# Output stage of a four-layer image network: spreading factors through masked copies and one product, row sums on VectorE, and both offsets' taps in one product

## Chip, cores and metric

The kernel runs on one core of a Trainium2 chip. The metric is the device time of one execution in microseconds (us), from one launch with all inputs in HBM to the output in HBM; the median over several executions is given. All data are float32.

## What is computed

The input is a batch of 4 images of 56 x 56 positions and 128 channels. Four layers follow one another:

- Layer 0: attention in shifted windows, attention over the whole image, and a two-layer perceptron.
- Layer 1: for each row of positions, sums of relu over all pairs of positions, then a linear layer with relu.
- Layer 2: an attention layer whose projections are spectral convolutions. It takes a sample as 56 images, one for each place t on the first axis, each of 56 (second axis) x 128 (channels) values. Its end is what matters here: each such image gets `attention = inorm(projd + xa)`, then `m = gelu(inorm(spec(inorm(attention))) + skip)`, `m = inorm(spec(m)) + skip`, and the output `inorm(m) + attention`. `inorm` takes mean and variance over one image's 56 x 128 values, so it has one factor for each t.
- Layer 3: a convolution with three taps along one image axis, and sums of its result over each axis.

Between layers 2 and 3 lies a normalization over groups of 4 channels, so layer 3's input is `r * (x - m)` per channel. Layer 3, cut to what matters:

```
y = conv(xc, W, taps along the first image axis, zero padding) + b
agent_sum = sum(y, axis=3)          # over the second image axis
time_sum  = sum(y, axis=2)          # over the first image axis
g = (agent_sum + time_sum - y) / sqrt(56 + 56 - 2)
out = relu(g + res)                 # res: the layer's input
```

A convolution of sums is the sum of the convolution, so the kernel convolves the sums of the input (`whole.nl`, over the second axis; `whole.na`, over the first) in place of summing the result. A sum over the first axis, shifted by one tap, lacks one edge row of the image: this is where the "row sums" of the change come in.

## The kernel before

Layers 0 to 2 run ahead of the stage that is changed. From about 3239 us on, `outputs` (L2624) does the end of layer 2 and the whole of layer 3. It works on four samples; each sample has two halves of 28 of its 56 images (`half_sample`, L2069), and then `last_layer` (L2431) runs once for the sample.

Both functions do not issue instructions at once. They add operations to a `Plan`: an operation has an engine, an estimated cost, the operations it comes after, and the buffers that it takes and gives back. `plan.issue` (L2048) then runs all 788 of them in the sequence `OUTPUT_ORDER` (L2591), a list of numbers written out in the source. Within an engine the instructions execute in that sequence, for TensorE, ScalarE, VectorE and GpSimd; between engines only semaphores order them. The change leaves the list as it is.

Buffers: `bank()` is one PSUM bank out of two (tag "b"), `banks()` a pair out of three (named `o_d`). GpSimd does not read PSUM here, so what it takes is copied by VectorE or ScalarE first.

**Spreading the factors.** In `half_sample` a tile is [128 partitions (channels), 28 images (T), 56 (second axis)]. An image belongs to one of four slots (t modulo 4) and one of seven groups (G = 7). `sums` forms the sums of squares of the images of slot s into partitions 32s to 32s + 31; `root` takes the square root on ScalarE and the reciprocal on VectorE (L2210). So one factor for each image stands in a small tile [128, G], in a different partition block for each slot. `everywhere` (L2213 to 2231) brings them to all 128 partitions. For each slot it multiplies with a stationary matrix `w.slot[:, s, :]`, which is 1 in the row 32s and 0 elsewhere:

```
for s in range(4):
    nc.tensor.matmul(ps[:, s * n * G:(s + 1) * n * G], w.slot[:, s, :],
                     V[src].rearrange("p x g -> p (x g)"), start=True, stop=True)
```

`copies` (L2229) then scales the result from PSUM into one value for each image. It happens twice for each half, 16 times in all:

- After `inverses` (L2303 the reciprocal, L2305 the small tile `o_e`), with two factors an image (n = 2). They become `f1` for `normed` (L2357, GpSimd) and `fs` for `skip` (L2317, GpSimd: `a = att * fs`).
- After the reciprocal of `r5` (L2210), with one factor an image. It becomes `f5` for `last` (GpSimd), behind which `sum2` (GpSimd) adds the half into the sample `whole.x`.

In between, `under` (L2312, VectorE) makes the factor `f` from `o_e`. L2110, L2127 and L2141 are the products of `over_h`, `over_c` and `over_w`; L2179 is the addition in `weighted` (GpSimd).

**The last layer.** For each sample: `aggregate` and `means` (L2462) and `variances` (L2475) give mean and variance of the channel groups; `root` takes the square root; `scale` takes the reciprocal (L2483) and multiplies the three tap matrices with it (`wr`, L2485). `over_l` (L2487 to 2495) forms on TensorE the sum of both halves of `whole.na`, three times in one PSUM bank, less an edge row for the first and the last tap, by eight products with the identity or its negative. `offsets` (L2497 to 2509, VectorE) scales and shifts `whole.nl` and those sums; L2506 makes the first offset, L2508 and L2509 make the second from PSUM. `over_taps` (L2516 and L2518) convolves the first offset with three products, and the second with three more. `rows` copies both results from PSUM. Then the sample is worked in pieces of 16 rows: `spread` (GpSimd), `convolve` (L2538, TensorE, needs `scale`), `add` (L2542, VectorE), `relu` (ScalarE), `store` (L2549, GpSimd, and a DMA).

Of the kernel before, what the change touches and what calls it, by code (L numbers as in the profile page):

```python
# [12 lines left out]
F32 = mybir.dt.float32  # L13
AF = mybir.ActivationFunctionType
ALU = mybir.AluOpType
# [4 lines left out]
P = 128  # L20
B = 4
HH = 56
# [2046 lines left out]
def half_sample(k, w, st, plan, b, half, whole, pools, rows, x2d, xm):  # L2069
# [4 lines left out]
    nc = k.nc  # L2074
# [11 lines left out]
    def tile_of(shape, tag):  # L2086
        return wk.tile(shape, F32, tag=tag, name="o_" + tag, bufs=plan.buffers.get(tag, 6))
# [5 lines left out]
    def op(engine, cost, after=(), takes=(), gives=(), **kw):  # L2093
        return lambda run: plan.add(engine, cost, run, after, takes, gives, **kw)
# [108 lines left out]
    def root(name, src, after, bias):  # L2203
# [6 lines left out]
            nc.vector.reciprocal(V[name], V[name])  # L2210
        return run, inverse

    def everywhere(src, n, after, outs):  # L2213

        bb, L = buf("b"), Env()

        @op("PE", 0.7, after, [bb])
        def run():
            L.ps = ps = bank()
            for s in range(4):  # L2220
                nc.tensor.matmul(ps[:, s * n * G:(s + 1) * n * G], w.slot[:, s, :], V[src].rearrange("p x g -> p (x g)"),
                                 start=True, stop=True)

        @op("DVE", 0.2 * n, [run], (), [bb])
        def copies():
            ps = L.ps[:, :4 * n * G].rearrange("p (s x g) -> p s x g", s=4, x=n)
            for i, (name, gain) in enumerate(outs):
                V[name] = tile_of([P, T], name)
                nc.vector.tensor_scalar_mul(V[name].rearrange("p (g s) -> p s g", s=4), ps[:, :, i, :], gain)  # L2229
        return copies  # L2230
# [70 lines left out]
    @op("DVE", 0.4, [roots])  # L2301
    def inverses():
        nc.vector.reciprocal(V.r, V.r)  # L2303
        V.e = tile_of([P, G], "e")
        nc.vector.tensor_scalar(V.e, V.s1, w.ec1, 1e-15, ALU.mult, ALU.add)  # L2305
    factors = everywhere("r", 2, [inverses], [("f1", w.ng[:, 1:2]), ("fs", w.g12m)])
# [91 lines left out]
    var = sums("r5", k.ones_px, "sq", HH, sqs, [sq])  # L2398
    rt, inv = root("r5", "r5", [var], k.eps)

    @op("DVE", 0.0, [inv])
    def view():
        V.r5x = V.r5.unsqueeze(1)
    factors = everywhere("r5x", 1, [view], [("f5", w.ng[:, 5:6])])
    whole.spread, whole.factors = (whole.spread if half else []) + [spread], factors
    for i in range(2):
        def last(i=i):
# [23 lines left out]
def last_layer(k, w, plan, b, whole, pools, out):  # L2431


    nc = k.nc
    wk, bank, banks = pools.wk, pools.bank, pools.banks
    V = Env()
    count = [0]

    def buf(n):
        count[0] += 1  # L2440
        return n, (b, count[0])

    def tile_of(shape, tag):
        return wk.tile(shape, F32, tag=tag, name="o_" + tag, bufs=plan.buffers.get(tag, 2))

    def op(engine, cost, after=(), takes=(), gives=(), **kw):
        return lambda run: plan.add(engine, cost, run, after, takes, gives, **kw)

    def flat():
        return whole.x.rearrange("p l a -> p (l a)")  # L2450

    b1, b2, b3 = buf("b"), buf("b"), buf("b")

    @op("DVE", 0.3, whole.done)
    def aggregate():
        V.mv = tile_of([P, 2], "mv")
        nc.vector.bn_aggr(V.mv, whole.gs.rearrange("p a b -> p (a b)"))

    @op("PE", 0.3, [aggregate], [b1])
    def means():  # L2460
        V.ps = bank()
        nc.tensor.matmul(V.ps[:, 0:1], k.g4, V.mv[:, 0:1], start=True, stop=True)  # L2462

    @op("DVE", 0.5, [means], (), [b1])
    def deviations():
        f = tile_of([P, 8], "lf")
        V.m, V.d, V.v, V.r, V.c, V.c55, V.c56, V.kb = (f[:, i:i + 1] for i in range(8))
        nc.vector.tensor_copy(V.m, V.ps[:, 0:1])
        nc.vector.tensor_scalar(V.d, V.mv[:, 0:1], V.m, None, ALU.subtract)
        nc.vector.tensor_scalar(V.v, V.d, V.d, V.mv[:, 1:2], ALU.mult, ALU.add)  # L2470

    @op("PE", 0.3, [deviations], [b2])
    def variances():
        V.pv = bank()
        nc.tensor.matmul(V.pv[:, 0:1], k.g4, V.v, start=True, stop=True)  # L2475

    @op("ACT", 0.3, [variances], (), [b2], table="sqrt")
    def root():
        nc.scalar.activation(V.r, V.pv[:, 0:1], AF.Sqrt, bias=k.eps)

    @op("DVE", 1.0, [root])
    def scale():
        nc.vector.reciprocal(V.r, V.r)  # L2483
        V.wr = tile_of([P, 3, P], "wr")
        nc.vector.tensor_scalar_mul(V.wr, w.Wr, V.r)  # L2485

    @op("PE", 1.5, [variances] + whole.sums, [b3])  # L2487
    def over_l():

        V.pn = bank()[:, :3 * HH].rearrange("p (t a) -> p t a", t=3)  # L2490
        for t, edge in enumerate((HH, None, 1)):
            nc.tensor.matmul(V.pn[:, t, :], k.ident, whole.na[:, 0, :], start=True, stop=False)
            nc.tensor.matmul(V.pn[:, t, :], k.ident, whole.na[:, 1, :], start=False, stop=(edge is None))
            if edge is not None:
                nc.tensor.matmul(V.pn[:, t, :], k.nident, whole.x[:, edge, :], start=False, stop=True)

    @op("DVE", 1.2, [scale, over_l], (), [b3])  # L2497
    def offsets():
        nc.vector.tensor_scalar(V.c, V.m, V.r, -1.0, ALU.mult, ALU.mult)
        nc.vector.tensor_scalar_mul(V.c55, V.c, HH - 1.0)  # L2500
        nc.vector.tensor_scalar_mul(V.c56, V.c, float(HH))
        nc.vector.tensor_scalar(V.kb, V.c, w.bs, None, ALU.add)
        V.nl = tile_of([P, HH + 2], "nlp")
        nc.vector.memset(V.nl[:, 0:1], 0.0)
        nc.vector.memset(V.nl[:, HH + 1:], 0.0)
        nc.vector.tensor_scalar(V.nl[:, 1:HH + 1], whole.nl, V.r, V.c55, ALU.mult, ALU.add)  # L2506
        V.na = tile_of([P, 3, HH], "nap")
        nc.vector.tensor_scalar(V.na[:, 0::2, :], V.pn[:, 0::2, :], V.r, V.c55, ALU.mult, ALU.add)  # L2508
        nc.vector.tensor_scalar(V.na[:, 1, :], V.pn[:, 1, :], V.r, V.c56, ALU.mult, ALU.add)  # L2509
    b4 = buf("b")  # L2510

    @op("PE", 1.5, [offsets], [b4])
    def over_taps():
        V.ps = ps = bank()
        for t in range(3):
            nc.tensor.matmul(ps[:, :HH], w.W[:, t, :], V.nl[:, t:t + HH], start=(t == 0), stop=(t == 2))  # L2516
        for t in range(3):
            nc.tensor.matmul(ps[:, HH:2 * HH], w.W[:, t, :], V.na[:, t, :], start=(t == 0), stop=(t == 2))  # L2518

    @op("DVE", 0.4, [over_taps], (), [b4])  # L2520
    def rows():
        V.s12 = tile_of([P, 2, HH], "s12")
        nc.vector.tensor_scalar(V.s12[:, 0, :], V.ps[:, :HH], V.kb, None, ALU.add)
        nc.vector.tensor_copy(V.s12[:, 1, :], V.ps[:, HH:2 * HH])
    pieces, whole.convolve = [(j, min(16, HH - j)) for j in range(0, HH, 16)], []
    for i, (j, n) in enumerate(pieces):
        d, o = buf("d"), buf("o")

        def spread(i=i, j=j, n=n):
            V["o%d" % i] = x = tile_of([P, 16, HH], "o")[:, :n]  # L2530
            nc.gpsimd.tensor_add(x, bc(V.s12[:, 0, j:j + n], 2, HH), bc(V.s12[:, 1, :], 1, n))

        def convolve(i=i, j=j, n=n):
            V["d%d" % i] = pd = banks()
            for u in range(n // 8):
                for t in range(3):
                    at = (j + 8 * u + t) * HH
                    nc.tensor.matmul(pd[:, u, :NB], V.wr[:, t, :], flat()[:, at:at + NB], start=(t == 0), stop=(t == 2))  # L2538

        def add(i=i, n=n):  # L2540
            o2 = V["o%d" % i].rearrange("p (u l) a -> p u (l a)", l=8)
            nc.vector.tensor_add(o2, o2, V["d%d" % i][:, :n // 8, :NB])  # L2542

        def relu(i=i):
            nc.scalar.activation(V["o%d" % i], V["o%d" % i], AF.Relu)

        def store(i=i, j=j, n=n):
            x = V["o%d" % i]
            nc.gpsimd.tensor_add(x, x, whole.x[:, 1 + j:1 + j + n, :])  # L2549
            nc.sync.dma_start(out[b][:, j:j + n, :], x)  # L2550
        p1 = plan.add("POOL", n / 10, spread, [rows], [o])
        p2 = plan.add("PE", 0.3 * n, convolve, [scale] + whole.done, [d])
        whole.convolve.append(p2)
        p = plan.add("DVE", 0.06 * n, add, [p1, p2], (), [d])
        p = plan.add("ACT", 0.055 * n, relu, [p])
        plan.add("POOL", 0.115 * n, store, [p], (), [o, ("x", b)], lag=3.0)
# [132 lines left out]
def build(k, packs, I, out):  # L2689
# [3 lines left out]
    with ExitStack() as es:  # L2693
# [100 lines left out]
        with tc.tile_pool(name="xh", bufs=1) as xp:  # L2794
# [19 lines left out]
            psum = es.enter_context(tc.tile_pool(name="l2_ps", bufs=2, space=PSUM))  # L2814
            attend(k, I, w2, st, dd, xat, xm, last_softmax, conv_weights(k, w2, l2p), psum)
            ats.close()
        w2.slot = es.enter_context(tc.tile_pool(name="slot", bufs=1)).tile([P, 4, P], F32, name="slot")
        nc.vector.tensor_copy(w2.slot, bc(k.ident[:, 0::32], 2, P))
        outputs(k, w2, st, ys, x2d, xm, out, psum)


# [19 lines left out]
```

## Time and profile before

| | |
|---|---|
| median of three executions | 3586.84 us (3580.55 to 3589.28) |
| the profiled execution | 3579.81 us |
| its span, first to last instruction | 3578.0 us |
| mean granted TensorE clock | 0.981 |
| busy: PE, DVE, ACT, POOL | 3372.0, 2702.3, 2089.9, 1249.2 us |
| the output stage in the span | 3239 to 3578 us |
| busy in it: PE, DVE, ACT, POOL | 313.0, 226.4, 144.2, 222.5 us |

PE is TensorE's products and PEld its weight loads, which overlap with them; DVE is VectorE, ACT ScalarE, POOL GpSimd. A line name such as L2221 is line 2221 of the kernel's source. A float32 product shows as two records (a pair of weight load and product twice). A group's line of the profile reads: line, engine, operation, output and input tiles, shapes, count, then busy us, mean ns of one, and the idle time in front. Where a line lists single instructions, the three numbers behind the count are the shortest, median and longest in ns. The chain of waits follows the work that ended last back from the last instruction, each step to what released it; a line of it is start, length, and what.

### The profile page before, as it was taken

The page shows a single profiled execution, that of the slowest core. Times are in us where ns is not written, and L with a number is a line of the kernel's source. Part 1 is how long each engine was busy: PE and PEld are TensorE (multiplying, and loading weights), DVE is VectorE, ACT ScalarE, POOL GpSimd, SP SyncE. Part 2 cuts the span into 40 slices and gives each one's busy share as a digit, 9 for nine tenths or more (in the row PEclk, how much of TensorE's full clock was granted, in tenths as well). Part 3 has the DMA queues.
Part 4 walks back from the last instruction along what each step waited for, and adds up shares of the span by engine and source line. Part 5 has one row for each costly group of instructions (what it writes and reads, how often), then busy time and mean ns, then how long its engine had stood idle before and what let it go on. Part 6 is the DMA issues. An engine that isn't in the chain of part 4 may idle for free.

```text
span 3578.0 us, 80873 instructions
## 1 busy us (share of the span) xinstructions
PE 3372.0 (94%) x36096; PEld 1549.4 (43%) x36096; DVE 2702.3 (76%) x2531; ACT 2089.9 (58%) x2103; POOL 1249.2 (35%) x752
## 2 busy tenths in 40 slices
PE   6999998989999898999999999999898899999998
PEld 4433344553333455333344643333456443336664
DVE  6588868767888696688859758887784678886776
ACT  4688865458888564688856458887552112214442
POOL 1000017600000581000018400000673778884686
PEclk8999999999999999999999999999998999999999
DMA  2144420014333000444310024442103027763101
GB/s 103 43 92 92 95 42 20 20 47 94 88 88 83 20 3 20 99 93 94 89 44 3 20 57 94 94 94 63 38 3 101 15 53 178 181 148 91 55 19 55
DMA packets 98076, 244.51 MB, mean 68 GB/s; under 512 B 64456, under 2 KB 69832, under 8 KB 92712
## 3 DMA queue, kind: packets, MB, share of 16 engines
q0 software_dynamic: 16128, 102.77, 14.2%
q1 hardware_dynamic: 74872, 123.64, 11.9%
q10 hardware_dynamic: 6720, 12.85, 1.3%
q8 instruction: 285, 4.67, 0.5%
q14 instruction: 71, 0.58, 0.1%
HBM read 79.46 MB, written 31.33 MB: 31 GB/s over the span
## 4 chain that ended last, share of the span: by engine, by line
PE 79%; DVE 10%; ACT 4%; issue 4%; POOL 3%; DMA 0%; POOLq 0%; DVEq 0%; ACTq 0%
PE f_pm L818 17%; PE f_pm L684 15%; PE u_po L1878 8%; PE e_acc L1238 7%; PE q_acc L1732 3%; DVE e_td L1231 3%; PE f_pm L791 2%; PE e_po L1206 2%; PE f_pm L770 2%; ACT f_ring L821 1%; PE f_pm L464 1%; PE o_d L2141 1%; DVE f_acc L673 1%; PE o_d L2538 1%; PE f_pm L715 1%
## 5 line engine op out<-in xcount | busy, mean ns | idle before, releaser
L821 ACT ACTIVATE f_ring<-f_pm 128x1792 f32<-128x1792 f32 (+1 forms) x764 | 1093.8, 1482 | 228.7 <-PE f_pm L818 181.2
L673 DVE TENSOR_TENSOR f_acc<-f_acc,f_ring 128x1792 f32<-128x1792 f32 x468 | 947.7, 2025 | 191.1 <-ACT f_ring L821 160.9
L818 PE MATMUL f_pm<-f_qT,f_kT 32*128 32x448 f32 x5376 | 725.2, 571 | 15.5 <-ACT f_ring L821 5.1
L684 PE MATMUL f_pm<-f_ring,f_va 128*32 128x448 f32 (+1 forms) x6304 | 589.4, 490 | 0.0
L663 POOL DMA_DIRECT2D f_far<-f_ring x112 | 96.6, 862 | 1329.3 <-ACT f_ring L821 1108.2
L1231 DVE TENSOR_TENSOR e_td<-e_pa,e_c 128x1792 f32<-128x1792 f32 x252 | 491.2, 2018 | 14.1 <-ACT e_a L1196 14.1
L1233 POOL TENSOR_TENSOR e_tp<-e_a,e_c 128x1792 f32<-128x1792 f32 x140 | 451.5, 3261 | 101.4 <-PE e_acc L1238 59.8
L818 PEld LDWEIGHTS f_pm<-f_qT,f_kT 32*128 32x128 f32 x5376 | 260.4, 183 | 417.2 <-ACT f_ring L821 304.7
L1238 PE MATMUL e_acc<-e_td,t_shared 32*32 32x448 f32 x8064 | 325.8, 545 | 24.9 <-DVE e_td L1231 24.0
L684 PEld LDWEIGHTS f_pm<-f_ring,f_va 128*32 128x32 f32 x6304 | 164.2, 109 | 409.7 <-issue 397.4
L1873 DVE TENSOR_TENSOR u_ud<-u_px,u_d 112x1792 f32<-112x1792 f32 x144 | 263.5, 1864 | 39.6 <-PE u_po L1878 35.4
L1235 ACT ACTIVATE e_tp<-e_tp 128x1792 f32<-128x1792 f32 x140 | 233.4, 1694 | 74.0 <-POOL e_tp L1233 74.0
L1875 POOL TENSOR_TENSOR u_up<-xh,u_d 112x1792 f32<-112x1792 f32 (+1 forms) x72 | 240.9, 3376 | 55.0 <-PE u_po L1878 39.7
L1238 PE MATMUL e_acc<-e_tp,t_shared 32*32 32x448 f32 x4480 | 222.6, 544 | 3.0 <-ACT e_tp L1235 2.4
L1878 PE MATMUL u_po<-u_ud,AT 112*64 112x448 f32 x1056 | 213.8, 544 | 1.9 <-DVE u_ud L1873 1.9
L1238 PEld LDWEIGHTS e_acc<-e_td,t_shared 32*32 32x32 f32 x8064 | 142.3, 103 | 138.4 <-DVE e_td L1231 79.4
L1878 PEld LDWEIGHTS u_po<-u_ud,AT 112*64 112x64 f32 x1056 | 74.4, 138 | 128.8 <-issue 112.9
L1250 ACT COPY e_sums<-e_acc 128x1792 f32<-128x1792 f32 x28 | 46.3, 1652 | 136.2 <-PE e_acc L1238 136.2
L1238 PEld LDWEIGHTS e_acc<-e_tp,t_shared 32*32 32x32 f32 x4480 | 96.5, 103 | 53.0 <-issue 16.6
L728 DVE RECIPROCAL f_den<-f_den 128x448 f32<-128x448 f32 x28 | 82.6, 2951 | 44.1 <-ACT f_den L725 44.1
L1717 POOL TENSOR_TENSOR q_u<-iS,q_g 128x1792 f32<-128x1792 f32 x32 | 102.8, 3236 | 23.0 <-PE q_acc L1732 22.8
L1732 PE MATMUL q_acc<-q_u,S 64*64 64x448 f32 x1024 | 104.6, 553 | 4.4 <-DVE q_u L1719 3.3
(525 smaller groups left out, 4511.6 us busy)
## 6 DMA issues: line engine op xcount, KB each, us to landing
f_far<-f_ring POOLq DMA_DIRECT2D x112, 896.0 KB, 6.3
u_d<-dd SPq DMA_DIRECT2D x46, 784.0 KB
f_far<-f_ring SPq DMA_DIRECT2D x28, 896.0 KB
xw<-in_x SPq DMA_DIRECT2D x4, 1568.0 KB
x2d<-x SPq DMA_DIRECT2D x4, 1568.0 KB
xat<-x SPq DMA_DIRECT2D x4, 1568.0 KB
x_xs<-xat ACTq DMA_DIRECT2D x32, 196.0 KB
xm<-x_ev ACTq DMA_DIRECT2D x64, 98.0 KB
```

The costliest lines, as they stand in the source:

```text
L673: nc.vector.tensor_add(e.acc, e.acc, slots(j, c))
L684: nc.tensor.matmul(e.po[heads[h], part], va[o, c, heads[h]], p, start=(c == 0), stop=(c == 23 and part.stop == NB))
L818: nc.tensor.matmul(ss[:, i, :NB], kT[heads[h], c * P:(c + 1) * P], qT[heads[h], blk(j)], start=True, stop=True)
L821: nc.scalar.activation(ring[:, slot:slot + m, :], ss[:, :m, :NB], AF.Exp, scale=scale)
L1231: nc.vector.tensor_tensor(t, am, cm, ALU.max)
L1233: nc.gpsimd.tensor_sub(t, bc(a.rearrange("p (l n) -> p l n", l=8), 1, 4), cm)
L1235: nc.scalar.activation(tf, tf, AF.Relu)
L1238: nc.tensor.matmul(acc[quarters[q], r, :NB], k.ident[o, o], t[o, q].rearrange("p l n -> p (l n)"), start=(g == 0), stop=(g == len(EDGE_TUR ...
L1732: nc.tensor.matmul(acc[bp][i][halves[hb % 2], hb // 2, :NB], x[o], u[o, 8 * hb:8 * hb + 8, :].rearrange("p h t -> p (h t)"), start=first, ...
L1873: nc.vector.tensor_mul(u, bc(px[:, :, :NB], 2, m), dm)
L1875: nc.gpsimd.tensor_mul(u, bc(x, 2, m), dm)
L1878: nc.tensor.matmul(po[64 * b2:64 * b2 + 64, :NB], st.AT[:, 8 * i + h0 + q, 2 * bp + b2, :], u[:, b2, q, :], start=(left == 16), stop=(left ...
```

## The change

`everywhere` no longer uses four stationary masks. A new step `masked`, on VectorE, multiplies the factors with a column mask (the identity's columns 0, 32, 64, 96), so that slot s of the copy holds the factors in partition 32s and zero elsewhere; one product with a matrix of ones then adds over the partitions, which spreads all four slots at once. For the first use, `masked` stands between the reciprocal and the small tile `o_e` within `inverses`; for the second it is the body of an operation of its own, in the place of one that issued no instruction. `over_l` becomes three VectorE operations with the result in SBUF, at the same number in the sequence, but on VectorE's queue. `offsets` puts both offsets into one tile with places 64 and 130 elements apart, such that one pattern with two blocks reads the right tap of each, and `over_taps` has three products with 112 columns. The tile of mask matrices, and the copy that filled it ahead of the stage, go.

```
+    def masked(src, n):
+        V.apart = x = tile_of([P, 4, n * G], "ap")
+        r = V[src].rearrange("p x g -> p (x g)") if n > 1 else V[src]
+        nc.vector.tensor_mul(x, bc(r, 1, 4), bc(k.ident[:, 0::32], 2, n * G))
+
     def everywhere(src, n, after, outs):
...
-            for s in range(4):
-                nc.tensor.matmul(ps[:, s * n * G:(s + 1) * n * G], w.slot[:, s, :], V[src].rearrange("p x g -> p (x g)"),
-                                 start=True, stop=True)
+            nc.tensor.matmul(ps[:, :4 * n * G], k.ones, V.apart.rearrange("p s g -> p (s g)"), start=True, stop=True)
...
     def inverses():
         nc.vector.reciprocal(V.r, V.r)
+        masked("r", 2)
         V.e = tile_of([P, G], "e")
...
-    @op("DVE", 0.0, [inv])
-    def view():
-        V.r5x = V.r5.unsqueeze(1)
-    factors = everywhere("r5x", 1, [view], [("f5", w.ng[:, 5:6])])
+    @op("DVE", 0.2, [inv])
+    def apart():
+        masked("r5", 1)
+    factors = everywhere("r5", 1, [apart], [("f5", w.ng[:, 5:6])])
...
-    b1, b2, b3 = buf("b"), buf("b"), buf("b")
+    b1, b2 = buf("b"), buf("b")
...
-    @op("PE", 1.5, [variances] + whole.sums, [b3])
+    @op("DVE", 0.5, [variances] + whole.sums)
     def over_l():
-        V.pn = bank()[:, :3 * HH].rearrange("p (t a) -> p t a", t=3)
-        for t, edge in enumerate((HH, None, 1)):
-            nc.tensor.matmul(V.pn[:, t, :], k.ident, whole.na[:, 0, :], start=True, stop=False)
-            nc.tensor.matmul(V.pn[:, t, :], k.ident, whole.na[:, 1, :], start=False, stop=(edge is None))
-            if edge is not None:
-                nc.tensor.matmul(V.pn[:, t, :], k.nident, whole.x[:, edge, :], start=False, stop=True)
-
-    @op("DVE", 1.2, [scale, over_l], (), [b3])
+        V.pn = tile_of([P, 3, HH], "pn")
+        nc.vector.tensor_add(V.pn[:, 1, :], whole.na[:, 0, :], whole.na[:, 1, :])
+        nc.vector.tensor_sub(V.pn[:, 0, :], V.pn[:, 1, :], whole.x[:, HH, :])
+        nc.vector.tensor_sub(V.pn[:, 2, :], V.pn[:, 1, :], whole.x[:, 1, :])
+
+    @op("DVE", 1.2, [scale, over_l])
     def offsets():
...
-        V.nl = tile_of([P, HH + 2], "nlp")
...
-        nc.vector.tensor_scalar(V.nl[:, 1:HH + 1], whole.nl, V.r, V.c55, ALU.mult, ALU.add)
-        V.na = tile_of([P, 3, HH], "nap")
-        nc.vector.tensor_scalar(V.na[:, 0::2, :], V.pn[:, 0::2, :], V.r, V.c55, ALU.mult, ALU.add)
-        nc.vector.tensor_scalar(V.na[:, 1, :], V.pn[:, 1, :], V.r, V.c56, ALU.mult, ALU.add)
+        V.n = tile_of([P, 7 * 64], "nap")
+        nl, ends = V.n[:, :HH + 2], V.n[:, 64:64 + 2 * 130].rearrange("p (b x) -> p b x", b=2)[:, :, :HH]
...
+        nc.vector.tensor_scalar(nl[:, 1:HH + 1], whole.nl, V.r, V.c55, ALU.mult, ALU.add)
+        nc.vector.tensor_scalar(ends, V.pn[:, 0::2, :], V.r, V.c55, ALU.mult, ALU.add)
+        nc.vector.tensor_scalar(V.n[:, 129:129 + HH], V.pn[:, 1, :], V.r, V.c56, ALU.mult, ALU.add)
...
-    @op("PE", 1.5, [offsets], [b4])
+    @op("PE", 0.8, [offsets], [b4])
     def over_taps():
         V.ps = ps = bank()
         for t in range(3):
-            nc.tensor.matmul(ps[:, :HH], w.W[:, t, :], V.nl[:, t:t + HH], start=(t == 0), stop=(t == 2))
-        for t in range(3):
-            nc.tensor.matmul(ps[:, HH:2 * HH], w.W[:, t, :], V.na[:, t, :], start=(t == 0), stop=(t == 2))
+            both = V.n[:, t:t + 128 * (t + 1)].rearrange("p (b x) -> p b x", b=2)[:, :, :HH]
+            nc.tensor.matmul(ps[:, :2 * HH].rearrange("p (b x) -> p b x", b=2), w.W[:, t, :], both,
+                             start=(t == 0), stop=(t == 2))
...
-        w2.slot = es.enter_context(tc.tile_pool(name="slot", bufs=1)).tile([P, 4, P], F32, name="slot")
-        nc.vector.tensor_copy(w2.slot, bc(k.ident[:, 0::32], 2, P))
```

More of the change, by code (lines that the diff above doesn't have):

```diff
@@ L2502, in offsets @@
         nc.vector.tensor_scalar(V.kb, V.c, w.bs, None, ALU.add)
-        V.nl = tile_of([P, HH + 2], "nlp")
-        nc.vector.memset(V.nl[:, 0:1], 0.0)
-        nc.vector.memset(V.nl[:, HH + 1:], 0.0)
-        nc.vector.tensor_scalar(V.nl[:, 1:HH + 1], whole.nl, V.r, V.c55, ALU.mult, ALU.add)
-        V.na = tile_of([P, 3, HH], "nap")
-        nc.vector.tensor_scalar(V.na[:, 0::2, :], V.pn[:, 0::2, :], V.r, V.c55, ALU.mult, ALU.add)
-        nc.vector.tensor_scalar(V.na[:, 1, :], V.pn[:, 1, :], V.r, V.c56, ALU.mult, ALU.add)
+        V.n = tile_of([P, 7 * 64], "nap")
+        nl, ends = V.n[:, :HH + 2], V.n[:, 64:64 + 2 * 130].rearrange("p (b x) -> p b x", b=2)[:, :, :HH]
+        nc.vector.memset(nl[:, 0:1], 0.0)
+        nc.vector.memset(nl[:, HH + 1:], 0.0)
+        nc.vector.tensor_scalar(nl[:, 1:HH + 1], whole.nl, V.r, V.c55, ALU.mult, ALU.add)
+        nc.vector.tensor_scalar(ends, V.pn[:, 0::2, :], V.r, V.c55, ALU.mult, ALU.add)
+        nc.vector.tensor_scalar(V.n[:, 129:129 + HH], V.pn[:, 1, :], V.r, V.c56, ALU.mult, ALU.add)
     b4 = buf("b")
-    @op("PE", 1.5, [offsets], [b4])
+    @op("PE", 0.8, [offsets], [b4])
     def over_taps():
```

## Prediction

> **What bounds the kernel now.** I read the page first, then the stretches of the output stage (3239 to 3578 us), then the chain of waits, then the costliest lines by form, and last the timeline around each edited step. The columns of a stretch are its length and then busy us (instructions) of PE, PEld, DVE, ACT and POOL, the granted clock, the DMA share and GB/s.
>
> ```profile
> PE 79%; DVE 10%; ACT 4%; issue 4%; POOL 3%; DMA 0%; POOLq 0%; DVEq 0%; ACTq 0%
> ```
> ```profile
> 3239.00:3388.00 149.00, 142.33 (x1087) 96.29 (x1086) 97.07 (x166) 73.22 (x109) 84.50 (x54) 1.00 0.27 70
> ...
> 3479.00:3515.00 36.00, 34.76 (x215) 22.09 (x214) 29.99 (x52) 11.45 (x14) 27.31 (x17) 1.00 0.11 45
> 3515.00:3519.00 4.00, 4.00 (x29) 2.18 (x22) 1.85 (x6) 0.30 (x1) 3.82 (x4) 0.57 0.02 6
> ...
> 3545.00:3578.00 33.00, 21.85 (x80) 12.62 (x80) 10.53 (x23) 5.88 (x8) 20.04 (x12) 0.88 0.21 84
> ```
>
> TensorE carries the stage until 3515: over the four stretches that make up 3239 to 3515 it is busy for 265.3 of 276 us, idle for 10.7. VectorE is next, at 83% from 3479 on, and GpSimd has stretches where it is nearly full. Behind 3545 there is a tail that nothing fills. So work taken off TensorE counts only where the chain runs through it, and what is added to VectorE is close to counting.
>
> ```profile
> 3347.73 0.99 PE o_b L2221 x8
> ...
> 3366.27 0.22 PE o_b L2495 x2
> ...
> 3369.71 0.81 PE o_b L2516 x6
> ```
>
> These chain lines (start, us, what) show edited products that carry the end. Of the 16 spreading products (L2221) only three stand on the chain (3296.50, 3347.73, 3466.65, for 0.85, 0.99 and 0.81 us). Two more (3263.48 and 3395.59) release GpSimd's product L2317, which the chain reaches. Of the four row-sum groups (L2492 to L2495) two do (they end at 3366.49 and at 3549.77, each 1.83 us after its start), and all four groups of taps (L2516, L2518).
>
> **What the change takes off TensorE.** A spread is now eight pairs of weight load and product in 0.87 to 1.06 us. After, it is one matmul, which the profile will show as two pairs; two pairs of this kind (L2475) take 0.25 to 0.31. Saved: 0.70 x 16 = 11.2 us. The row sums, 16 pairs, take 1.83 us and go: 7.3 us for four samples. The taps are 12 pairs in 1.50 us and become 6 pairs with twice the columns; 6 pairs of 56 columns take 0.67 to 0.81 and 14 pairs of 112 columns take 1.73 (L2110), so 6 of these 0.74. Saved: 0.75 x 4 = 3.0. In all 21.5 us of TensorE's work.
>
> On the chain: spreads 0.6 + 0.7 + 0.6 = 1.9; the two ahead of GpSimd 2 x 0.7 = 1.4; row sums 2 x 1.83 = 3.66; taps 3.0. That is 10.0 us if nothing takes their place.
>
> **What it puts on VectorE.** Sixteen products of a broadcast factor with a mask column (eight of 128x56, eight of 128x28) and twelve additions or subtractions of 128x56, all with both inputs in SBUF. The nearest rows of the whole trace are:
>
> ```profile
> L1471 DVE TENSOR_TENSOR s_d<-s_d 128x56 f32<-128x56 f32 x4 | 0.9, 213 | 0.1
> ...
> L1458 DVE TENSOR_TENSOR s_t<-s_mv,s_mr 128x1 f32<-128x1 f32 x4 | 5.9, 1483 | 0.1
> L2675 DVE TENSOR_TENSOR gf_t<-gf_mv,gf_mr 128x1 f32<-128x1 f32 x4 | 0.6, 160 | 0.1
> ```
>
> L1472 of the same size takes 250. So 0.22 us each, 28 x 0.22 = 6.2 us. The copy that built the old mask matrices goes (0.42 us at 3235.4, before the stage, beside TensorE's work: nothing). The last two lines show the other side: the same 128x1 operation takes 160 ns in one place and 1483 in another. In the output stage it is seen in the open:
>
> ```profile
> L2312 DVE SCALAR_TENSOR_TENSOR o_f<-o_f,factors,o_e x8: 226/344/3287, 3269.4 to 3477.9; 128x7 f32<-128x7 f32 x8
> L2305 DVE TENSOR_SCALAR o_e<-o_s,factors x8: 147/149/2719, 3260.7 to 3466.1; 128x7 f32<-128x7 f32 x8
> ```
> ```profile
> 3265.09 2.81 POOL L2317 TENSOR_TENSOR o_a<-o_t,o_fs 128x1568 f32<-128x1568 f32 x1 [2.24 <-ACT o_r L2299]
> 3265.21 2.72 DVE L2305 TENSOR_SCALAR o_e<-o_s,factors 128x7 f32<-128x7 f32 x1
> ...
> 3334.27 3.29 DVE L2312 SCALAR_TENSOR_TENSOR o_f<-o_f,factors,o_e 128x7 f32<-128x7 f32 x1
> 3334.69 2.85 POOL L2357 TENSOR_TENSOR o_t<-o_t,o_f 128x1568 f32<-128x1568 f32 x1
> ```
>
> The three numbers are the shortest, median and longest in ns. A 7-element VectorE operation ends within 0.03 us of GpSimd's 1568-element product, twice. L2508, which reads PSUM, takes 382 to 391 ns every time. So a small VectorE operation on SBUF data alone can last as long as the GpSimd operation it meets. [...]
>
> **Where the masked copies meet GpSimd.** Each stands directly behind its reciprocal (L2303 or L2210) and ahead of L2305, and the product waits for it. I looked up GpSimd at the 16 moments. It is idle or in a memset at seven, at one (3260.69) the copy gets in just ahead, and at eight it is in a long product or starts one. What that costs on the path:
> - The copies' own 0.22 at the five spreads where the chain or GpSimd's next product hangs on them: +1.1.
> - 3265.21: GpSimd holds until 3267.90, the product that ran from 3266.68 to 3267.74 runs from about 3268.1 to 3268.35. That is +0.6 where 0.7 was to be saved: +1.3 against the sum above (it also eats the lead of the spread ahead of it).
> - 3466.11: GpSimd starts at 3466.12, and lasts until 3468.22. If the copy loses, the product at 3466.65 ends at about 3468.65 instead of 3467.46: +1.8 against its gain of 0.6; taken at half, +0.9.
> - 3476.6, 3481.4 and 3529.4: the block ends by 3478.28, 3481.89 and 3530.30, about when the product starts today; what they eat is off the chain. 3398.33, 3405.22, 3412.48: the chain is GpSimd's there (busy for 39.48 of 46 us from 3388 to 3434), nothing.
> - L2305 is pushed back by the copy and can meet the next GpSimd product: 1.5 to 3 us of VectorE at one or two places; half of 1.5 on the path, +0.7.
>
> Bounds of this block term: zero if the copies always win, and 16 x 0.6 (the mean excess of L2312, 832 less its shortest 226) = 9.6 us if each loses as often as L2312. I take the itemised sum, 1.1 + 1.3 + 0.9 + 0.7 = 4.0. The spreads thus come to -3.3 + 4.0 = +0.7.
>
> **Row sums and taps.** The offsets (L2499 to L2509) now need three more VectorE operations in front, 0.65 us in VectorE's order, and the taps need all offsets where the first three products needed only the first.
>
> ```profile
> 3369.64 0.88 PE L2516 MATMUL o_b<-o_nlp,t_w_W 128*128 128x56 f32 x6
> 3369.75 0.33 DVE L2509 TENSOR_SCALAR o_nap<-o_b,o_lf 128x56 f32<-128x56 f32 x1
> ```
>
> VectorE is writing its last offset (until 3370.08) when TensorE begins the taps. Sample 0: 1.83 us of row sums leave TensorE, but the offsets end 0.65 later (3370.73), and the taps end at 3370.73 + 0.74 = 3371.5 against 3371.2 before: +0.3. Samples 1 and 2: the chain already runs through the offsets, +0.65 - 0.75 = -0.1 each. Sample 3: the convolution starts at 3549.77, the scaled weights are ready at 3549.01 and become so at 3549.66: the row sums' gain is void, the taps give -0.65. The sum is 0.3 - 0.2 - 0.65 = -0.55, not the -6.7 of the chain's pieces. Moving the last sums from PSUM to SBUF as the offsets' source is worth under 0.1 each, and may add a meeting with GpSimd in the tail (L2549, 3549.22 to 3550.35): bounds 0 and +0.8. One PSUM bank less is asked for per sample; TensorE waits for banks nowhere on the chain lines here, so nothing.
>
> **Sum.** +0.7 - 0.55 = +0.15 us. On the profiled execution's 3579.8 (span 3578.0 and 1.8 around it) that is 3580; it lay 7.0 below the median of 3586.84, so the forecast is 3587.
>
> **Rivals.** *TensorE stays the bound, faster.* For it: only 10.7 us idle in 276, and GpSimd is free at half the moments. Then the chain's 10.0 is the least; of the 21.5, 4.0 lie behind 3515 (two spreads, one row sum, one set of taps), so 17.5 at most before that. The middle, 13.7, gives 3573. Against it: 3369.64, where VectorE finishes with no slack at all. It holds from the point where the masked copies end before TensorE reaches their product at most places.
>
> *VectorE blocked by GpSimd, slower.* All 16 copies fall on the path with the L2312 excess: 16 x (0.22 + 0.6) = 13.1, less 3.3, +9.8; the row sums 4 x 0.65 - 3.0 = -0.4; and TensorE's new waits at three samples' ends each bring a stretch at half clock.
>
> ```profile
> 3515.30 2.65 PE o_d L2127 x16
> ```
>
> That group takes 1.53 us elsewhere; it ran where the clock was granted at 0.57, after pauses of TensorE: 1.1 a time, 3.3 in all. Together +12.7, which is 3600. It decides from the point where the copies end later than TensorE reaches their product, that is from about 0.7 us of blocking each. Against it: the clock is 1.00 everywhere before 3515.
>
> *The change doesn't do what it says* (still eight pairs in a spread): unlikely, as the instruction order shows one matmul; it would be +6 by VectorE's new work, inside the forecast's bounds.
>
> **How the numbers follow.** 0.3% of the median is 10.8 us, about what a measurement of this kernel can tell from no change. The forecast's case (gains eaten, within 3576 to 3597) gets 0.43; the faster rival 0.27, because idle TensorE time is so small that more than the chain's pieces may shrink; the slower one 0.30, because so many short operations are exposed. The range reaches from 3570 (the faster rival with 17 of 17.5) to 3604 (the slower one with another clock dip and the 0.8 at the tail, and some drift of the median); about 1 in 10 is left out at each side.
>
> **What would show it.** Right: L2221's group at 32 records, TensorE busy some 20 us less, yet idle in front of the spreads with VectorE's copy as releaser; copies with a median near 0.22 us and a few over 1; the taps released by the offsets. The faster rival: the stretch to 3515 shorter by 10 or more, copies all near 0.22. The slower one: mean of the copies over 0.8 us, more stretches with a clock under 1. The forecast is wrong if the end moves by over 10.8 us, most of all if the copies hardly ever meet GpSimd.

## The result, and the profile after

| | before | changed |
|---|---|---|
| median of seven runs | 3584.13 us (3580.09 to 3589.28) | 3595.99 us (3593.94 to 3601.82) |
| profiled execution, its span | 3579.81, 3578.0 us | 3601.82, 3600.0 us |
| mean granted clock in it | 0.981 | 0.973 |

The changed kernel takes 1.0037 times as long (95% interval 1.0025 to 1.0049): 11.9 us slower by the medians. That is inside the range, between the forecast (3587) and the slower rival (3600). As a change, +11.9 us lies next to the slower rival's +12.7, and it is more than the 10.8 us (0.3%) that the prediction had named as the sign that its forecast is wrong. The profiled execution is the slowest of the seven, so its 22 us are more than the usual difference; about 5 us of them arise ahead of the output stage, which starts 5.1 us later in this trace.

From the page of the changed kernel, span and busy times:

```profile
span 3600.0 us, 80528 instructions
...
PE 3380.0 (94%) x35912; PEld 1542.6 (43%) x35912; DVE 2714.8 (75%) x2558; ACT 2090.0 (58%) x2103; POOL 1249.7 (35%) x752
```

TensorE executes 184 products fewer than the 36,096 of before: 96 from the spreading, 64 from the row sums, 24 from the taps, which is what the diff says. Yet it is busy for 8 us longer. The reason is in the column of the granted clock (the third from the end) of the stage's stretches:

```profile
3260.00:3280.00 20.00, 18.49 (x122) 11.04 (x118) 15.24 (x23) 6.87 (x12) 11.41 (x6) 0.86 0.02 4
3280.00:3300.00 20.00, 18.52 (x146) 13.30 (x142) 10.02 (x21) 14.21 (x22) 4.59 (x5) 0.84 0.37 139
...
3340.00:3360.00 20.00, 18.48 (x130) 11.70 (x130) 17.31 (x24) 9.58 (x14) 17.19 (x9) 0.83 0.20 41
...
3520.00:3540.00 20.00, 15.27 (x94) 9.00 (x95) 16.82 (x37) 6.11 (x9) 13.00 (x8) 0.83 0.15 58
3540.00:3560.00 20.00, 15.33 (x57) 6.61 (x54) 14.72 (x24) 4.06 (x6) 14.62 (x10) 0.83 0.01 1
```

In the trace of before, all five of these stretches stand at 1.00, and one stretch alone in the stage ahead of the last 10 us was at half clock (granted 0.50, 3515.6 to 3519). In the changed kernel there are eight, and each lasts 3.4 or 6.8 us. Full speed lost to them is 1.7 us before and 23.9 us after.

The edited operations, by line (count, then shortest/median/longest in ns), and the idle time of TensorE in front of the two new products (last columns):

```profile
L2217 DVE TENSOR_TENSOR o_ap<-o_r,t_shared x16: 186/603/2155, 3265.9 to 3549.2; 128x56 f32<-128x56 f32 x8, 128x28 f32<-128x28 f32 x8
L2310 DVE TENSOR_SCALAR o_e<-o_s,factors x8: 218/223/1486, 3267.9 to 3483.6; 128x7 f32<-128x7 f32 x8
L2521 PE MATMUL o_b<-o_nap,t_w_W 128*128 128x112 f32 x24 | 4.9, 359 | 7.8 <-DVE o_nap L2511 7.8
L2226 PE MATMUL o_b<-o_ap,c_ones 128*128 128x28 f32 x16 | 3.3, 289 | 3.8 <-DVE o_ap L2217 3.7
```

The 16 masked copies (L2217) sum to 13.3 us, against 3.2 us at their shortest. The timeline shows the first two, which cost over 2 us each (start, length, engine, line):

```profile
3265.82 2.08 POOL L2179 TENSOR_TENSOR o_y<-o_t,o_t 112x896 f32<-112x896 f32 x1 [20.76 <-DVE o_t L2170]
3265.92 2.05 DVE L2217 TENSOR_TENSOR o_ap<-o_r,t_shared 128x56 f32<-128x56 f32 x1
...
3269.70 2.81 POOL L2322 TENSOR_TENSOR o_a<-o_t,o_fs 128x1568 f32<-128x1568 f32 x1 [1.81 <-ACT o_t L2183]
...
3270.43 2.15 DVE L2217 TENSOR_TENSOR o_ap<-o_r,t_shared 128x56 f32<-128x56 f32 x1
...
3272.74 0.40 PE L2226 MATMUL o_b<-o_ap,c_ones 128*128 128x56 f32 x2 [1.51 <-DVE o_e L2310]
```

Each copy ends 0.07 us after GpSimd's instruction (3267.97 behind 3267.90, 3272.58 behind 3272.51). TensorE has 1.51 us of idle time ahead of the second product, and 1.7 us after that the clock halves (3274.4). So the blocked copies, priced one by one in the forecast, are real. The other place is the end of a sample, here sample 1 (samples count from 0):

```profile
3451.35 2.09 POOL L2179 TENSOR_TENSOR o_y<-o_t,o_t 112x896 f32<-112x896 f32 x1 [4.42 <-DVE o_lf L2488]
3451.37 2.27 DVE L2490 TENSOR_SCALAR o_wr<-Wr,o_lf 128x384 f32<-128x384 f32 x1
...
3453.57 0.20 DVE L2496 TENSOR_TENSOR o_pn<-o_na 128x56 f32<-128x56 f32 x1
...
3454.07 1.84 DVE L2331 TENSOR_TENSOR o_a<-o_a,o_d 128x784 f32<-128x784 f32 x2
...
3457.04 1.59 PE L2521 MATMUL o_b<-o_nap,t_w_W 128*128 128x112 f32 x6 [3.25 <-DVE o_nap L2511]
```

The scaled taps (L2490, 420 ns when alone) lie beside GpSimd for 2.27 us, then come the three row sums, an addition of another half (L2331), and only then the offsets. TensorE stands idle for 3.25 us, and the taps that follow take 1.59 us in place of the 0.92 of sample 0; the clock is halved from 3455.3 on.

### The profile page after: what moved, and what is told of

Its sections match the earlier page's. It is cut to its first block, busy times and chain, and to the rows that moved or that the text cites. A ratio compares the mean times of both kernels' runs of the same rounds, so it can differ in the third digit from the quotient of the medians.

```text
span 3600.0 us, 80528 instructions
## 1 busy us (share of the span) xinstructions
PE 3380.0 (94%) x35912; PEld 1542.6 (43%) x35912; DVE 2714.8 (75%) x2558; ACT 2090.0 (58%) x2103; POOL 1249.7 (35%) x752
## 4 chain that ended last, share of the span: by engine, by line
PE 78%; DVE 11%; ACT 4%; issue 4%; POOL 3%; DMA 0%; POOLq 0%; DVEq 0%; ACTq 0%
PE f_pm L818 17%; PE f_pm L684 15%; PE u_po L1878 8%; PE e_acc L1238 7%; PE q_acc L1732 3%; DVE e_td L1231 3%; PE f_pm L791 2%; PE e_po L1206 2%; PE f_pm L770 2%; ACT f_ring L821 1%; PE o_d L2542 1%; PE f_pm L464 1%; PE o_d L2141 1%; DVE f_acc L673 1%; PE s_pr L1527 1%
```

## Theories

Theory A: the loss is the copies' blocking, with the clock's answer to the waits. Theory B: it is the row sums and taps, for which TensorE now waits at each sample's end. A third reading came up on the way: the waits themselves cost little, and the half clock behind them most of the loss.

For each kernel two numbers are given beside the ratio. *Lost* is the span times one less its mean granted clock; *rest* is the span less that. Both are means over all runs of a kernel, as differences from the before of the same session (lost 69.2 to 70.7 us, of which 61.4 of 67.1 lie ahead of the stage in the trace of before; rest 3511.7 to 3512.5). For the changed kernel the before of spreads_only's session stands in. The standard error of a difference is 1 to 3 us for lost and about 1 us for rest. A trace is of one execution: those of rows_taps and after_psum are of the fastest of their runs.

| kernel | ratio to before (95%) | lost | rest |
|---|---|---|---|
| changed | 1.0037 (1.0025 to 1.0049) | +20.2 | -6.3 |
| spreads_only | 1.0026 (1.0016 to 1.0035) | +10.4 | -2.0 |
| spreads_psum | 1.0017 (1.0007 to 1.0028) | +8.5 | -3.2 |
| rowsums_only | 1.0031 (1.0021 to 1.0042) | +12.4 | -1.1 |
| taps_only | 0.9998 (0.9989 to 1.0007) | +1.3 | -1.7 |
| rows_taps | 1.0024 (1.0014 to 1.0034) | +13.0 | -5.3 |
| rows_taps_act | 1.0005 (0.9995 to 1.0014) | +6.2 | -4.5 |
| after_psum | 1.0030 (1.0021 to 1.0039) | +14.4 | -4.5 |
| after_psum_act | 1.0012 (1.0003 to 1.0021) | +10.2 | -5.6 |
| after_fill | 1.0018 (1.0010 to 1.0027) | +0.9 | +5.3 |
| wr_act | 0.9987 (0.9978 to 0.9997) | -3.7 | -0.7 |
| taps_act | 1.0005 (0.9996 to 1.0013) | +6.7 | -5.0 |
| psum_taps_act | 0.9994 (0.9985 to 1.0003) | +6.3 | -7.8 |

The two must not be read as price and saving, since lost time is not paid in full. Over the 235 executions whose mean clock is on record, compared within each kernel and session, one with 10 us more lost is about 6.2 us longer, so rest falls by itself where lost rises. The first line is the answer in short: TensorE loses 20.2 us more of full speed. At 0.62 of that, 12.5 of the 13.9 us between the means are the clock's, and some +1 us is left for all else (an estimate from the same runs). The 6.3 us by which rest fell are thus no shown saving.

## The experiments

**spreads_only**: before, with `masked`, the one product with ones, and `apart`; row sums, offsets and taps as they were.

```
+    def masked(src, n): ...
-            for s in range(4): matmul(..., w.slot[:, s, :], ...)
+            nc.tensor.matmul(ps[:, :4 * n * G], k.ones, V.apart...)
```

> The kernel before with the spreading alone changed (16 masked copies on VectorE, one product with ones each); row sums and taps as before. Theory A (the copies lie blocked behind GpSimd's instructions, TensorE waits for them, and the clock halves after the waits): most of the loss is here, +6 to +12 us against before; the 16 copies together take over 8 us where 3.3 would do, and at least three half-clock stretches lie ahead of the tail. Theory B (the loss comes from the row sums and taps, for which TensorE now waits on VectorE's offsets at each sample's end): -4 to +1 us, one half-clock stretch ahead of the tail.

Measured: 3592.13 us, +8.5 by the medians. The copies sum to 13.5 us, and its trace has exactly three half-clock stretches ahead of the tail. A holds for this half of the change.

**rows_taps**: the other half of the diff, `over_l` on VectorE and `over_taps` in three products, spreading as before.

> The kernel before with the row sums on VectorE and the taps in one product, the spreading as before. Theory A: -3 to +3 us against before. Theory B: +6 to +12 us, with gaps of 1.5 to 3 us in front of the taps and a half-clock stretch behind each.

Measured: 3590.3 us, +6.6 by the medians and +8.6 by the ratio. That is B's number, so neither theory alone is right: both halves lose, each about two thirds of the whole. The gaps in front of the taps of samples 0 to 2 are 1.57, 2.54 and 3.05 us; at sample 3 the gap, 1.83 us, lies in front of the convolution. Rest fell by 5.3 us and lost rose by 13.0.

**after_psum**: the changed kernel, with the square roots in PSUM at 13 of the 16 spreads; at the other three they stay in SBUF. The bank is then held from the square root on, longer than before, which is a second difference.

```
-        V.r = tile_of([P, 2, G], "r")
+        V.rb = bank()
+        V.r = V.rb[:, 64:64 + 2 * G]...        # then reciprocal and masked copy read PSUM
```

> The changed kernel, but the square roots are written to a PSUM bank (at 13 of the 16 spreads), so the reciprocal and the masked copy read PSUM and the copy has one SBUF input. Theory A: the 13 copies take 0.2 to 0.35 us each, none over 0.6, and the time is 5 to 12 us under the changed kernel's. Theory B: copies short too, but the time within 3 us of the changed kernel's.

The copies, by the tile that they read (o_b is PSUM):

```profile
L2218 DVE TENSOR_TENSOR o_ap<-o_b,t_shared x13: 186/189/217, 3258.1 to 3533.0; 128x28 f32<-128x28 f32 x7, 128x56 f32<-128x56 f32 x6
L2218 DVE TENSOR_TENSOR o_ap<-o_r,t_shared x3: 186/218/231, 3308.8 to 3433.4; 128x56 f32<-128x56 f32 x2, 128x28 f32<-128x28 f32 x1
```

No copy is blocked any more: 3.2 us for all 16. Nine of the 13 ran while GpSimd was in an instruction on SBUF, and were as short as the others: the longest of the 13 took 217 ns, where the changed kernel's copies from SBUF took up to 2155 ns. That shows what the long copies were: copies that lay beside a GpSimd instruction until its end, with both sources in SBUF. But VectorE is not free by it:

```profile
3257.97 2.08 POOL L2179 TENSOR_TENSOR o_y<-o_t,o_t 112x896 f32<-112x896 f32 x1 [20.75 <-DVE o_t L2170]
3258.09 0.22 DVE L2218 TENSOR_TENSOR o_ap<-o_b,t_shared 128x56 f32<-128x56 f32 x1
3258.22 1.86 DVE L2313 TENSOR_SCALAR o_e<-o_s,factors 128x7 f32<-128x7 f32 x1
```

The next instruction in the queue, the small tile `o_e`, now lies blocked until 3260.08, and so at three places (1.86 to 1.88 us each; over its shortest it takes 5.3 us in all, against 1.5 in the changed kernel). The time is 3592.09 us, about 4 under the changed kernel, between the two expectations and within the noise (the intervals of the two ratios overlap). What the blocked copies cost the kernel is therefore not measured by this run.

**after_fill**: the changed kernel with idle products added, whose results nobody reads.

```
+            for u in range(3):      # in front of each spreading product
+                nc.tensor.matmul(ps[:, 128 + 64 * u:128 + 64 * u + 56], k.ones, k.ident[:, :56], ...)
+        for u in range(8):          # in front of each sample's taps
+            nc.tensor.matmul(ps[:, 128:128 + HH], k.ones, k.ident[:, :HH], ...)
```

> The changed kernel with products that nobody reads added on TensorE: three of 56 columns in front of each spreading product, eight in front of each sample's taps, 80 in all or about 18 us of TensorE work, placed where it would wait. If the waits cost mainly by the half clock behind them: fewer half-clock stretches than in the changed kernel (eight ahead of the tail) and 4 to 12 us less time in spite of the added work. If the waits themselves are the cost, or TensorE's work is: within 2 us of the changed kernel, or up to 10 us slower.

```profile
L2227 PE MATMUL o_b<-t_shared,c_ones 128*128 128x56 f32 x96 | 13.7, 279 | 0.0
L2522 PE MATMUL o_b<-t_shared,c_ones 128*128 128x56 f32 x64 | 7.8, 275 | 0.0
...
3260.00:3570.00 310.00, 290.37 (x2048) 186.56 (x2045) 232.15 (x410) 132.51 (x183) 213.56 (x128) 0.99 0.15 48
```

With 160 records of idle work, the clock of the stage is 0.99 (the changed kernel's from 3262 to 3580 is 0.92), two half-clock stretches remain of eight, lost is back at +0.9, and the kernel is about 7 us *faster* than without that work (3589.11 us; its runs reach from 3586 to 3596, the changed kernel's from 3594 to 3602). The copies are as blocked as before (186/606/2684 ns). This is the run that decides between the readings: added work can't shorten a wait, so the gain is the clock's, and what the waits cost is mainly the half clock behind them. Rest is 5.3 us over before's: the fill, with 21.5 us of products, isn't free, and the waits that are left are in that number too.

**taps_only**: three products of 112 columns in place of six of 56, the row sums still from TensorE and in PSUM.

> The kernel before with both offsets' taps in one product, row sums on TensorE and spreading as before. If the taps' wait for all offsets is what opens the gaps at the sample ends: most of the loss of the row-sum part (+4 to +8 us against before), gaps of 1 us and more in front of the taps. If it is the row sums' going from TensorE to VectorE's queue: -2 to +2 us.

Measured: 3583.62 us, no difference. The first expectation failed: the taps' wait is 1.9 us in sum over the samples, and before had 1.6.

**rowsums_only**: `over_l` alone on VectorE.

> The kernel before with the row sums alone moved from TensorE to VectorE; taps in six products, spreading as before. By the runs so far (both +7 us, taps alone 0) the row sums carry the loss: +5 to +9 us against before, with gaps at the sample ends and lost clock time some 8 to 14 us over before's. If it takes the two together (taps that wait for offsets that are late): -2 to +3.

Measured: 3592.65 us, +10.2 by the medians, 1.0031 by the ratio; lost +12.4. So the row sums are the whole of that half's loss; the taps change nothing that these runs can tell (1.0024 with them).

**rows_taps_act**: rows_taps, with the instruction that lay in front of the offsets moved off VectorE.

```
-        nc.vector.tensor_scalar_mul(V.wr, w.Wr, V.r)
+        nc.scalar.activation(V.wr, w.Wr, AF.Identity, scale=V.r)
```

> Row sums on VectorE and taps in one product, spreading as before, and the scaled taps (wr) made on ScalarE instead of VectorE, where the instruction lay blocked for 2.1 to 2.3 us at three of four samples. If the gaps at the sample ends are that blocked instruction in front of the offsets: the gaps before the taps of samples 1 to 3 shrink from 1.5 to 3 us to under 1, fewer half-clock windows than rows_taps, and -5 to +1 us against before. If the row sums themselves delay the offsets: within 2 us of rows_taps (+7).

```profile
3437.65 2.13 POOL L2179 TENSOR_TENSOR o_y<-o_t,o_t 112x896 f32<-112x896 f32 x1 [4.16 <-DVE o_lf L2483]
3437.67 0.62 ACT L2485 ACTIVATE o_wr<-Wr,o_lf 128x384 f32<-128x384 f32 x1 [0.68 <-DVE o_lf L2483]
3437.79 2.06 DVE L2492 TENSOR_TENSOR o_pn<-o_pn,o_x 128x56 f32<-128x56 f32 x1
```

Measured: 3585.8 us, ratio 1.0005 (rows_taps had 1.0024), a little over the expected +1. On ScalarE the same multiplication takes 0.62 us beside the same GpSimd addition. But the gaps in front of the taps of samples 0 to 2 are 0.68, 2.03 and 2.18 us, not all under 1, and the third line says why: a row sum behind it in VectorE's queue now lies blocked in its place, for 2.06 us (the row sum after that one, L2493, takes 0.20). At samples 0 and 2 it is the first offset (L2505, about 1.47 us in place of 0.31). Moving one instruction away handed the meeting to one behind it.

**wr_act**: the same edit alone, in the kernel before.

> The kernel before with the scaled taps made on ScalarE and nothing else changed. The chain of before runs through the offsets at samples 1 and 2, behind the blocked instruction: -1 to -5 us if the wait is on the chain; within 1 us of before if TensorE's row sums (1.83 us a sample) cover it.

```profile
L2485 ACT ACTIVATE o_wr<-Wr,o_lf x4: 599/614/616, 3370.8 to 3550.2; 128x384 f32<-128x384 f32 x4
```

Measured: 3580.0 us, -4.1, ratio 0.9987 (0.9978 to 0.9997). This is the one version here that beats both kernels beyond its interval. The block is handed on here too, but to a shorter one: the first offset (L2506) takes 1.50 and 1.48 us at samples 0 and 2, where alone it takes 0.31, and ends with GpSimd's addition; the scaled taps had taken 2.2 to 2.3 us at three samples. TensorE's idle time in front of the taps falls from 1.6 to 0.2 us, and the trace has no half-clock stretch ahead of the tail, against one in that of before.

**after_psum_act**: the whole change with masked copies and scaled taps unblocked.

> The whole change, with the masked copies reading PSUM and the scaled taps made on ScalarE, so neither is blocked by GpSimd. If blocked VectorE instructions, through waits and the half clock behind them, are the cause of the loss: -8 to -1 us against before, and lost clock time (span times one less the mean clock) within 6 us of before's 69. If the change loses because TensorE with less work has more idle time whatever it waits for, and the clock answers to that: +3 to +9 us, lost clock time 75 to 85.

Measured: 3587.87 us, 1.0012, lost +10.2 (80.9 us). The kernel still loses, with lost time as the second expectation has it.

```profile
L2511 DVE TENSOR_TENSOR o_pn<-o_pn,o_x x4: 216/628/2022, 3371.5 to 3556.7; 128x56 f32<-128x56 f32 x4
L2524 DVE TENSOR_SCALAR o_nap<-o_nl,o_lf x4: 309/1110/1447, 3373.6 to 3557.7; 128x56 f32<-128x56 f32 x4
```

But the run does not decide between the two, since VectorE is not unblocked: a row sum (L2511) and the first offset (L2524) lie blocked in place of the scaled taps, and `o_e` as in after_psum. TensorE still waits 0.63, 2.84 and 2.15 us in front of the taps of samples 0 to 2. That the loss goes back to blocked instructions alone is neither shown nor refuted.

**spreads_psum**: spreads_only with unblocked copies.

> The spreading alone changed, as in spreads_only, with the masked copy reading PSUM at 13 of 16 places. If the blocked copies are the whole of the spreading's loss (+8.5 us): -4 to +1 us against before, lost clock time within 4 us of before's. If the spreading loses mostly because TensorE, with 11 us less work, waits for other engines in the same places and the clock answers: +3 to +8 us, copies all near 0.2 us.

Measured: 3585.55 us, ratio 1.0017, lost +8.5, copies at 186 to 225 ns. The second expectation's number holds: with short copies, too, the new spreading loses. Why stays open, as `o_e` is blocked here as in after_psum and the banks are held longer. Five of its twelve runs took 3591 to 3597 us at a mean clock of 0.975 to 0.976, the other seven 3579 to 3586 us at 0.980 to 0.981. The profiled execution (span 3580.9) is of the seven, and has no half-clock stretch ahead of the tail. So how much half clock occurs differs from run to run of one kernel, and the loss itself is in no trace.

**taps_act** and **psum_taps_act**: taps in one product and scaled taps on ScalarE, row sums on TensorE; the second also with the new spreading reading PSUM.

> A version that may beat both kernels: taps in one product, row sums on TensorE, spreading as before, scaled taps made on ScalarE. From wr_act (-4.1 us) and taps_only (-0.5 us): -3 to -7 us against before if the two add, -1 to -4 if TensorE's saved 0.75 us a sample turns into waits.

> As taps_act, with the new spreading and the masked copies reading PSUM. If unblocked copies make the spreading a gain: 1 to 5 us under taps_act. If less work on TensorE means more half-clock windows: 2 to 7 us over taps_act, with lost clock time 75 to 82.

Measured: 3585.17 us (1.0005) and 3581.42 us (0.9994), neither clear of before. taps_act failed on both expectations: the gain of wr_act does not come back, and lost rose by 6.7. The second is 3.8 under the first, as its first expectation has it, but their intervals overlap; its rest is the shortest of all, -7.8, with lost at +6.3.

What came ahead of the half clock can be read in taps_act, where a half-clock stretch begins at 3412.4 with no gap in front of it (length, then busy PE, PEld, DVE, ACT, POOL, then the clock):

```profile
3405.20:3408.60 3.40, 3.40 (x36) 3.09 (x35) 1.93 (x3) 1.68 (x3) 3.32 (x3) 1.00 0.00 0
3408.60:3412.00 3.40, 3.40 (x34) 2.96 (x26) 2.22 (x5) 3.38 (x4) 3.40 (x3) 1.00 0.00 0
3412.00:3415.40 3.40, 3.40 (x17) 2.65 (x17) 3.40 (x6) 1.89 (x5) 3.40 (x2) 0.56 0.97 200
```

TensorE is busy without a break, but with products of 7 and 64 columns, each behind a weight load of 128. What can be counted is columns: the sum, over TensorE's records in a window, of the columns each streams, a record that crosses an edge shared out by its time. The eight starts of half-clock stretches in the changed kernel's trace (3274.4, 3294.9, 3346.1, 3383.6, 3455.3, 3530.4, 3547.5, 3571.4) lie whole multiples of 3.413 us apart, within 0.1 us (the first and the last 296.96 us, 87 times 3.4133), and so do those of every other trace here. For the count each trace is cut into windows of that length, from its own starts. Of the windows at full clock in all 14 traces, from 3200 us to 10 us before the end:

| columns in the window | windows | next one at half clock |
|---|---|---|
| under 1600 | 28 | 26 |
| 1600 to 2050 | 66 | 7 |
| over 2050 | 1359 | 8 |

The window ahead of 3412.4 has 1511 columns. TensorE was busy for over 90% of 1156 of these windows, and half clock followed behind three of them, all with under 1600 columns. The count is a correlation over traces, with bounds chosen on the same traces, and not without exceptions, as the table shows; that filling the waits restores the clock is shown by after_fill (0.99 in place of 0.92).

## Why the prediction was right and wrong, by its steps

- *What is taken off TensorE.* Right in counts (184 records). Of the 10.0 us on the chain no saving is shown: rest fell by 6.3 us, but that is what it does where lost rises by 20. The busy time "some 20 us less" was wrong: it rose by 8.0, because products took longer at half clock (the taps of sample 1 1.59 us, those of sample 0 0.92).
- *VectorE's new operations.* 0.2 us each when alone: right (186 to 231 ns).
- *Meetings with GpSimd.* Right in kind; in number nine of 16 copies took over 0.6 us, where eight places had been named. The mean of 0.83 us is the slower rival's 0.82, not the forecast's median near 0.22. The spreading, forecast at +0.7 us, measured +8.5 alone, with 10.4 more lost. The term of 4.0 us can't be compared with a run: unblocking the copies changed the time by about 4 us, within the noise, and handed the block to the instruction behind.
- *Row sums and taps, -0.55 us.* This step failed: the row sums alone measured +10 us, with 12.4 more lost and rest no longer than before. It moved three operations into VectorE's order at 0.65 us and counted TensorE's 1.83 us as freed, without asking what TensorE would do in that time. It had nothing else to do then: it reaches the taps earlier, and the offsets come later. In before, the scaled taps lay blocked in front of the offsets for 2.2 to 2.3 us at three samples (L2485, 420/2180/2328 ns); the row sums lay just ahead of that at sample 0, inside it at sample 1 and for the most part ahead of it at sample 2, and TensorE waited 0, 0.56 and 1.08 us in front of the taps. In the changed kernel it waits 1.53, 3.25 and 3.05. The gain of the taps in one product, 3.0 us on the chain, is neither shown nor excluded (-0.5 us, within the noise).
- *The clock.* The term that was mis-sized most: zero in the forecast, 3.3 us in the slower rival, and +20.2 us lost in the runs, worth about 12.5 us of time. The reason to set it at zero, that the clock was 1.00 everywhere before 3515, told how before behaves, and nothing about what new waits would do to it.
- *The rivals.* The faster one was refuted: the time rose, and even rest fell by less than half of its 13.7 us. The slower one came near in its number (+12.7 against +11.9), and both of its signs were seen, the copies' mean and more stretches under full clock. Its parts fit less well: the spreading's +9.8 and the 3.3 for the clock (three stretches of 1.1 us, where the trace has 14 windows of 1.7) against +8.5 measured with the clock in it, and the row sums and taps at -0.4 against +6.6. So its closeness is partly luck.
- *The forecast.* Its +0.15 us did not happen. That the time lies inside the range is owed to the slower rival's end of it. The work as a whole may have come out near nothing, as the sum had it (some +1 us by the estimate above); what the sum lacked is the clock.
- *One PSUM bank less*: nothing seen, as expected.

## What to carry to other kernels

Before products are taken off a busy TensorE, ask what TensorE will do in their time: work that fills a wait is not a saving when it goes (the row sums' 1.83 us a sample, taken off TensorE alone, gave +10 us), and here most of the price came from the clock behind the wait (12.5 of 13.9 us, by the estimate above). Count what TensorE streams in each 3.4 us, not only whether it is busy (in these traces the count told more: half clock followed 26 of 28 windows with under 1600 columns, but only 38 of the 297 in which TensorE was busy for 90% or less), and keep short products and waits from falling together. Where a small VectorE instruction shows a time that a GpSimd instruction's end explains, give it a PSUM source (the masked copies then took at most 217 ns, in place of up to 2155) or move it to ScalarE (the scaled taps then took 0.62 us, in place of up to 2.33), and look at which instruction behind it is next to be blocked.

## Not expected of the hardware

- In each of these traces the half-clock stretches begin whole multiples of 3.413 us apart, and one followed a window with few streamed columns where TensorE was busy all through (1511 columns, 3409.0 to 3412.4 in taps_act).
- Adding 160 product records to a stage made it about 7 us faster.
- ScalarE's multiplication of 128x384 takes 0.61 us beside a GpSimd addition, VectorE's 0.42 us alone and up to 2.33 us beside one; where one VectorE instruction was unblocked, one behind it was held (a row sum for 2.06 us in rows_taps_act, a tile of 7 elements for 1.86 us in after_psum).
